# Expert routing and the last sums of a Perceiver block on one core: filler products between the counts, ranks in PSUM, earlier last adds and writes

## The chip, the cores and the metric

The kernel runs on one core of a Trainium2 chip. The metric is the device time of one execution in microseconds, the median of several runs. The profile is one execution of its own, recorded by the hardware profiler; its times are given from the start of the span.

## The reference

The reference takes two latents of 256 rows and 256 channels each (512 tokens in all) and two contexts of 4096 rows of 128 channels, in float32. Six layers follow each other, each with a residual: cross attention, a state-space layer, a spectral layer, a second cross attention, a sparse self attention, and a mixture of experts. The change lies in the last of them:

```python
x = x + _L1_ffn_ref(_layernorm(x, axis=-1), L1_ffn_W1, L1_ffn_W2, L1_ffn_Wr)

E, DFF, TOPK = (8, 1024, 2)
logits = jnp.einsum('btd,ed->bte', x, Wr)
probs = jax.nn.softmax(logits / TEMPERATURE, axis=-1)
topk_vals, topk_idx = jax.lax.top_k(probs, TOPK)
router_weights = topk_vals / topk_vals.sum(-1, keepdims=True)
one_hot = jax.nn.one_hot(topk_idx, E, dtype=x.dtype)
gate = jnp.einsum('btk,btke->bte', router_weights, one_hot)
h = jax.nn.silu(jnp.einsum('btd,efd->btef', x, W1))
y = jnp.einsum('btef,edf->bted', h, W2)
out = jnp.einsum('bte,bted->btd', gate, y)
```

## The kernel before

The first five layers fill the span up to about 730 us. An order written out by hand (the string `ORDER`) weaves the work of the two latents together there; while `in_order[0]` is true, calls through the wrappers `te`, `ve` and `se` (TensorE, VectorE, ScalarE) keep their program order, and the profile gives all of them the line of the wrapper, L172. The part that follows, L1313 to L1579, is mostly written with plain `nc.` calls, which a scheduler orders on each engine.

The 512 tokens lie as four tiles (`NT` = 4) of 128 rows. The router's products (`ps_r`) give eight logits for each token. The selection (L1327 to L1337) is a chain of small VectorE operations: twice the greatest logit, as a mask `sel`, and their sum `picked`, 128 x 4 x 8. For each token and expert the rank of the token among those that chose the expert is needed. TensorE multiplies `picked` by a matrix of ones (totals of a tile) and by `above`, a strict triangle (tokens ahead in the tile), both into one bank `ps_n` (L1343, L1344); VectorE adds the totals up over the tiles into `cum` (L1349) and then `pos` (L1351). `cum[:, NT, :]` is the number of tokens of each expert.

The work of the experts is cut into blocks of 128 tokens. Block k below 8 holds the first 128 tokens of expert k; further blocks hold what is over. Twelve blocks (`ALWAYS` = 12) are always worked on; three more stand under the condition at L1569, which reads `filled`, and were not needed in these runs. `direct(k)` gathers the tokens of blocks 0 to 2 by a product: a comparison of `count` with `number` makes a 0/1 matrix S of 128 x 512 (L1367), and eight products of `xn5` with it give the block, turned (`ps_xs`, L1374). The tokens of all blocks are also scattered to `x_slots` in DRAM by eight indirect DMAs on GpSimd's queue (L1406), at places computed by VectorE (`slot`, `two`, `both`, `at`). From block 3 on, ScalarE's queue fetches a block from there (L1454) and TensorE turns it (L1459).

Each block goes through `hidden` (`ps_h`, L1466, with Silu on ScalarE at L1473) and `output` (`ps_y`, L1482). The results of blocks 0 to 9 are stored to `y_slots` (L1491); those of blocks 10 and 11 stay on the core and are spread over the tokens by products with `SHARES` (`combine`, L1515, added to x by VectorE at L1520). After block 9, `collect` reads each token's two results back with eight indirect DMAs on GpSimd's queue (L1527), and VectorE adds each row to x with its weight (L1531). The weights of the experts come on SyncE's queue (L1262, L1263). The last four DMAs write x out, two on SyncE's queue and two on ScalarE's (L1579); they stand behind the condition.

## Time and profile before

| what | value |
|---|---|
| time, median of 3 runs (lowest to highest) | 852.71 us (852.42 to 853.16) |
| the profiled execution: its own time, its span | 855.07 us, 853.3 us |
| granted TensorE clock, mean of the span | 0.979 |
| busy: PE, PEld, DVE, ACT, POOL | 801.2, 572.7, 581.5, 451.8, 46.3 us |
| share of the chain that ended last: PE, DVE, ACT | 82%, 10%, 4% |
| router's last product ends; selection's last mask starts | 738.57 us; 741.28 us |
| direct products, 48 instructions | 744.71 to 752.73 us |
| first of eight gathers starts; last one starts | 834.62 us; 843.48 us |
| writes of x issued from | 848.98 us |

PE is TensorE's products, PEld its loads of weights, DVE is VectorE, ACT ScalarE, POOL GpSimd, SP SyncE; a "q" behind a name is the engine's queue, which also issues DMAs. One product of 128 x 128 weights in float32 shows as two instructions. Busy time tells how long an engine worked, not that it was waited for; the chain that ended last tells which work the end stood behind. "Granted clock" is the share of TensorE's full clock in a stretch.

### The profile page before, as it was taken

To read this page: it belongs to the slowest core of one execution; us is meant where nothing else is said; L and a number is where in the kernel's file an instruction comes from. 1 tells how busy PE (TensorE), PEld (TensorE's weight loads), DVE (VectorE), ACT (ScalarE), POOL (GpSimd) and SP (SyncE) were. 2 spreads that over 40 slices of the span, in tenths; PEclk is the share of its full clock that TensorE was granted. 3 is DMA by queue.
4 is the path that set the end of the run, shared out by engine and by line. 5 is a ranking of instruction groups with operands and counts; after the bars stand their busy time and mean duration, and the time that the engine had idled before them with its cause. 6 is when DMAs were issued, how large, how long until landed. Compare 5 with 4: busy or idle time off the path is not lost.

```text
span 853.3 us, 20944 instructions
## 1 busy us (share of the span) xinstructions
PE 801.2 (94%) x8596; PEld 572.7 (67%) x8596; DVE 581.5 (68%) x1072; ACT 451.8 (53%) x858; POOL 46.3 (5%) x108
## 2 busy tenths in 40 slices
PE   5998999999999999999988999989799999699996
PEld 3675666666666666666655666865668865599985
DVE  4686888887878787687798766888774587631112
ACT  6434666666666666566654787655534244311110
POOL 5004011000000000000000000000000000030003
PEclk9997999999999999999999999999999999699998
DMA  7215114001101010100000101130305502339502
GB/s 269 55 35 181 25 39 124 17 20 23 23 17 24 11 30 18 22 14 15 2 2 2 51 2 49 53 99 1 99 2 196 196 2 68 132 111 330 200 13 82
DMA packets 35313, 56.65 MB, mean 66 GB/s; under 512 B 5872, under 2 KB 22816, under 8 KB 35216
## 3 DMA queue, kind: packets, MB, share of 16 engines
q1 hardware_dynamic: 27904, 41.44, 16.0%
q0 software_dynamic: 3264, 10.05, 3.5%
q10 hardware_dynamic: 4048, 3.80, 1.6%
q8 instruction: 69, 1.13, 0.6%
q14 instruction: 28, 0.23, 0.1%
HBM read 42.16 MB, written 4.85 MB: 55 GB/s over the span
## 4 chain that ended last, share of the span: by engine, by line
PE 82%; DVE 10%; ACT 4%; issue 2%; DMA 1%; POOL 1%; POOLq 0%; ACTq 0%; DVEq 0%
PE ps L172 29%; PE av L172 17%; PE ps_h L1466 5%; PE ps_y L1482 4%; PE ps_k L172 4%; PE ps_v L172 3%; PE ps_s L172 3%; DVE mp L172 3%; DVE states L172 2%; PE ps_aqk L172 2%; PE ps_in L172 2%; PE ps_pt L172 1%; PE ps_f L172 1%; PE ps_ht L172 1%; PE asc L172 1%
## 5 line engine op out<-in xcount | busy, mean ns | idle before, releaser
L172 DVE TENSOR_REDUCE mp<-ps 128x2 f32<-128x1024 f32 (+1 forms) x273 | 303.1, 1153 | 96.7 <-PE ps L172 96.6
L172 ACT ACTIVATE exps<-ps 128x512 f32<-128x512 f32 x512 | 266.6, 602 | 131.0 <-PE ps L172 130.7
L172 PE MATMUL ps<-qk,KB 32*128 32x256 f32 x2048 | 260.7, 397 | 3.4 <-ACT exps L172 1.7
L172 PE MATMUL ps<-KB,qk 32*128 32x256 f32 x2048 | 251.4, 395 | 4.5 <-DVE mp L172 4.5
L172 PEld LDWEIGHTS ps<-KB,qk 32*128 32x128 f32 x2048 | 172.9, 186 | 60.2 <-issue 34.0
L172 PEld LDWEIGHTS ps<-qk,KB 32*128 32x128 f32 x2048 | 187.8, 186 | 18.1 <-ACT exps L172 5.2
L172 PE MATMUL av<-exps,V 128*32 128x256 f32 x2048 | 136.8, 385 | 1.2 <-ACT exps L172 0.8
L172 PEld LDWEIGHTS av<-exps,V 128*32 128x32 f32 x2048 | 53.7, 109 | 63.5 <-ACT exps L172 33.2
L172 DVE TENSOR_TENSOR av<-av 128x256 f32<-128x256 f32 x120 | 49.5, 412 | 5.4 <-PE av L172 5.0
L1473 ACT ACTIVATE room<-ps_h 128x512 f32<-128x512 f32 x24 | 14.2, 597 | 72.6 <-PE ps_h L1466 51.4
L1466 PEld LDWEIGHTS ps_h<-room,w 128*128 128x128 f32 x384 | 44.5, 192 | 0.5
L1466 PE MATMUL ps_h<-room,w 128*128 128x128 f32 x384 | 44.7, 275 | 0.0
L1482 PE MATMUL ps_y<-w,room 128*128 128x256 f32 x192 | 43.3, 379 | 0.0
L172 PEld LDWEIGHTS ps_v<-l_wv,ctxT 128*128 128x128 f32 x256 | 32.6, 191 | 15.2 <-issue 6.6
L172 DVE TENSOR_TENSOR_SCAN states<-decay,ps_in 128x256 f32<-128x256 f32 x64 | 40.0, 669 | 2.5 <-PE ps_in L172 2.5
L1482 PEld LDWEIGHTS ps_y<-w,room 128*128 128x128 f32 x192 | 35.6, 190 | 4.4
L172 PE MATMUL ps_k<-ctxT,wkc 128*128 128x512 f32 x64 | 36.5, 655 | 0.0
L172 PE MATMUL av<-more,nat 128*128 128x256 f32 x128 | 33.4, 384 | 3.0 <-DVE more L172 2.8
L172 PE MATMUL ps_v<-l_wv,ctxT 128*128 128x128 f32 x256 | 35.0, 280 | 1.0 <-ACT V L172 1.0
L172 ACT COPY qk<-ps_k 128x512 f32<-128x512 f32 x32 | 18.7, 587 | 26.8 <-PE ps_k L172 25.1
L172 PE MATMUL ps_s<-ctxT,xn 128*128 128x512 f32 x64 | 29.5, 594 | 0.0
L172 ACT COPY V<-ps_v 128x512 f32<-128x512 f32 x32 | 18.8, 587 | 20.1 <-PE ps_v L172 15.1
(308 smaller groups left out, 854.6 us busy)
## 6 DMA issues: line engine op xcount, KB each, us to landing
w<-in_moe_w SPq DMA_DIRECT2D x24, 1024.0 KB, 7.6
KB<-qk SPq DMA_DIRECT2D x220, 32.0 KB, 2.0
ctxT<-in_ctxT SPq DMA_DIRECT2D x4, 512.0 KB, 7.8
ctxT<-in_ctxT POOLq DMA_DIRECT2D x4, 512.0 KB, 5.1
x_slots<-O POOLq DMA_DIRECT2D x15, 128.0 KB, 6.2
y_slots<-room ACTq DMA_DIRECT2D x10, 128.0 KB, 4.2
room<-x_slots ACTq DMA_DIRECT2D x9, 128.0 KB, 5.2
KB<-qk ACTq DMA_DIRECT2D x32, 32.0 KB, 2.2
```

Source lines behind the costliest of these rows:

```text
L172: i = getattr(self.engine, name)(*args, **kw)
L1466: nc.tensor.matmul(ps[fc // 4][:, (fc % 4) * P : (fc % 4 + 1) * P], lhsT=weights[k][0][:, c, fc * P : (fc + 1) * P], rhs=xT[k][:, c, :], s ...
L1473: nc.scalar.activation(hT[k][:, 4 * i : 4 * i + 4, :].rearrange("p f n -> p (f n)"), ps[i], AF.Silu)
L1482: nc.tensor.matmul(ps[:, :D], lhsT=hT[k][:, fc, :], rhs=weights[k][1][:, fc, :], start=(fc == 0), stop=(fc == NF - 1),)
```

## The change

Eight products of a constant row with the identity, read by nobody (`at_work(8)`), stand between the router's products and the counts, and four more (`at_work(4)`) between the counts and the direct products. The ranks are summed in PSUM: `picked` gets a fifth slice of zeros, and five products that accumulate in one bank give `pos` and the number of tokens `num` at once; `cum` and its adds are gone. S is made in four comparisons of 128 x 128 for each block in place of one of 128 x 512. These products keep their program order. At the end, `collect` issues the gathers and returns the adds; seven of the eight adds come first, then the combined results, then the eighth add, in that order on VectorE. x is written ahead of the condition, and inside it once more for the case that it is taken.

```diff
+        picked = one.tile([P, NT + 1, E], F32, tag="picked", name="picked")
+        nc.vector.memset(picked[:, NT, :], 0.0)
+        def at_work(n):
+            ps = bank("ps_work")
+            for _ in range(n):
+                te.matmul(ps[:, :D], lhsT=ident, rhs=rows[:, LN_G, :], start=True, stop=True)
...
-        nc.vector.tensor_add(picked, sel[:, 0, :, :], sel[:, 1, :, :])
-        flat = picked.rearrange("p t e -> p (t e)")
+        nc.vector.tensor_add(picked[:, :NT, :], sel[:, 0, :, :], sel[:, 1, :, :])
+        in_order[0] = True
+        at_work(8)
         ps = bank("ps_n")
-        nc.tensor.matmul(ps[:, : NT * E], lhsT=ones, rhs=flat, start=True, stop=True)
-        nc.tensor.matmul(ps[:, NT * E : 2 * NT * E], lhsT=above, rhs=flat, start=True, stop=True)
-        tot = ps[:, : NT * E].rearrange("p (t e) -> p t e", e=E)
-        cum = one.tile([P, NT + 1, E], F32, tag="cum", name="cum")
-        nc.vector.memset(cum[:, 0, :], 0.0)
+        te.matmul(
+            ps[:, : (NT + 1) * E], lhsT=above, rhs=picked.rearrange("p t e -> p (t e)"), start=True, stop=False
+        )
         for t in range(NT):
-            nc.vector.tensor_tensor(cum[:, t + 1, :], cum[:, t, :], tot[:, t, :], ALU.add)
-        pos = one.tile([P, NT, E], F32, tag="pos", name="pos")
-        nc.vector.tensor_tensor(
-            pos, cum[:, :NT, :], ps[:, NT * E : 2 * NT * E].rearrange("p (t e) -> p t e", e=E), ALU.add
-        )
+            te.matmul(
+                ps[:, (t + 1) * E : (NT + 1) * E].rearrange("p (t e) -> p t e", e=E), lhsT=ones,
+                rhs=picked[:, t : t + 1, :].to_broadcast([P, NT - t, E]), start=False, stop=(t == NT - 1),
+            )
+        at_work(4)
+        pos = ps[:, : NT * E].rearrange("p (t e) -> p t e", e=E)
+        num = ps[:, NT * E : (NT + 1) * E]
...
-            nc.vector.tensor_tensor(
-                S, count.unsqueeze(1).to_broadcast([P, NT, P]),
-                number[:, :, k : k + 1].to_broadcast([P, NT, P]), ALU.is_equal,
-            )
+            for t in range(NT):
+                nc.vector.tensor_single_scalar(S[:, t, :], count, number[:, t, k : k + 1], ALU.is_equal)
...
-                    nc.tensor.matmul(
+                    te.matmul(
                         ps[:, c * P : (c + 1) * P], lhsT=xn5[:, t, c * P : (c + 1) * P], rhs=S[:, t, :],
...
         direct(0)
-        num = cum[:, NT, :]
+        in_order[0] = False
...
-        def collect():
-            for i in range(TOP_E):
-                for t in range(NT):
+        def collect(i, t):
...
+            def added():
+                ve.scalar_tensor_tensor(x[:, t, :], row, kept[:, i, t : t + 1], x[:, t, :], ALU.mult, ALU.add)
+            return added
...
-                collect()
+                rows_of.extend(collect(i, t) for i in range(TOP_E) for t in range(NT))
...
+        in_order[0] = True
+        for added in rows_of[:-1]:
+            added()
         combine((STORED, STORED + 1))
+        rows_of[-1]()
+        in_order[0] = False
+        write()
         with tc.If(nc.values_load(filled[0:1, :], min_val=0, max_val=E - 1) > ALWAYS - E):
...
             blocks(ALWAYS, NB, add_up)
-        for t in range(NT):
-            (nc.scalar if t % 2 else nc.sync).dma_start(out=out[t * P : (t + 1) * P, :], in_=x[:, t, :])
+            write()
```

## The prediction

> **What bounds the kernel now.** I read the page first. In it the chain that ended last is PE for 82% of the span, so time is won only where that chain leaves PE at full speed, or at its ends. The change touches two places: the routing (about 738 to 753 us) and the last ten microseconds. The next view is the chain of waits in order of time for 736 to 775 us (start, length, what):

> ```profile
> 741.61 0.61 PE ps_n L1343 x2
> 742.22 0.44 PE ps_n L1344 x2
> ...
> 743.96 0.60 DVE gathered L1367
> ...
> 744.71 8.01 PE ps_xs L1374 x48
> 752.73 7.15 PE ps_h L1466 x64
> 759.87 3.46 PE ps_y L1482 x16
> ```

> DVE picks the experts until 741.5 us, PE counts for 1.05 us, DVE ranks and compares for 2.0 us, and from 744.71 us PE is the chain. Its first 48 instructions (the direct products, 128 columns) take 8.01 us, or 167 ns each; the 64 behind them, of the same shape, take 112 ns. The view by windows says why (columns: stretch, length, busy time of PE, PEld, DVE, ACT, POOL, then the granted clock, DMA share, GB/s):

> ```profile
> 732.00:734.00 2.00, 1.17 (x6) 1.12 (x7) 1.61 (x6) 0.20 (x1) 0.00 (x0) 0.68 0.41 131
> ...
> 748.00:749.00 1.00, 1.00 (x7) 1.00 (x6) 0.43 (x2) 0.00 (x0) 0.00 (x0) 0.50 0.00 0
> 749.00:750.00 1.00, 1.00 (x8) 1.00 (x8) 0.90 (x7) 0.00 (x0) 0.00 (x0) 0.61 0.00 0
> 750.00:751.00 1.00, 1.00 (x12) 1.00 (x10) 0.14 (x3) 0.00 (x0) 0.67 (x1) 1.00 0.00 0
> ```

> What follows the routing, from the timeline (start, length, engine, line, operation):

> ```profile
> 749.87 0.17 DVE L1402 CAST at<-both 128x8 int32<-128x8 f32 x1
> ...
> 750.33 1.05 POOL L1406 DMA_INDIRECT x_slots<-xn,at  x1 [83.52 <-DVE known L1448]
> ...
> 762.20 1.32 ACTq L1454 DMA_DIRECT2D room<-x_slots  x3
> ...
> 766.74 0.38 PE L1459 MATMUL ps_xs<-ident,room 128*128 128x128 f32 x2
> ```

> The scatters start when the slots are known, the fetches on ACT's queue wait for all eight, and PE needs the first fetched block at 766.74 us. And the end:

> ```profile
> 845.13 0.48 DVE L1531 SCALAR_TENSOR_TENSOR x<-gathered,kept,x 128x256 f32<-128x256 f32 x1 [0.82 <-DMA gathered<-y_slots,known]
> 847.09 0.48 DVE L1531 SCALAR_TENSOR_TENSOR x<-gathered,kept,x 128x256 f32<-128x256 f32 x1 [1.48 <-DMA gathered<-y_slots,known]
> 847.49 1.41 DVE L1520 TENSOR_TENSOR x<-x,ps_c 128x256 f32<-128x256 f32 x4
> 848.98 0.85 SPq L1579 DMA_DIRECT2D out_x<-x  x2
> 848.99 0.88 ACTq L1579 DMA_DIRECT2D out_x<-x  x2
> ```

> The eighth gathered row sets the end; the four combined adds wait behind it although their products were done at 845.45 us; then four writes, two on each queue.

> **Routing, step by step.** (1) The eight products stand on PE directly behind the router's, which end at 738.57 us. Each is two instructions of 256 columns: 16. At full clock ps_y shows 3.46/16 = 0.216 us for one, at half clock 0.43 (the 256-wide scores between 73.6 and 76.3 us, at clock 0.50, stand 0.43 apart). On this run's grid the next full step is 739.54 to 742.96 us, so 4.4/0.43 = 10.2 instructions are slow and 5.8 x 0.216 = 1.25 us fast: PE is free at 744.2 us. The selection that this work lies beside ends at 741.5 us, so 2.7 us stick out on the path.

> (2) The ranks: five products, ten instructions of at most 40 columns. They cost what the weight load costs, taken from warm ps_xs (its last 16 instructions, 750.98 to 752.73 us: 0.109 us each): 1.1 us, and 0.2 us until DVE sees the last: 745.5 us, against 742.66 before. Gone are the four dependent adds and the position add on DVE, 742.68 to 743.54 us.

> (3) The four products behind the ranks: 8 x 0.216 = 1.7 us, PE free at 747.0 us. Meanwhile DVE makes `number` (0.2 us) and the first four compares, now one for each tile. The nearest row is L1500, four 128x128 in 1.10 us: all four are there at 745.5 + 0.2 + 1.2 = 746.9 us, just covered; were they half as slow again, PE would wait about 0.4 us. The other eight compares alternate with eight small operations (0.26 + 0.08 us a pair), ending at 749.6 us; PE needs the third block at 747.0 + 3.5 = 750.5 us.

> (4) The direct products, all at full clock: 48 x 0.109 = 5.25 us, ending at 752.3 us against 752.73. That is -0.4 us. Where the grid falls in another execution is open: a lag of one step (3.4 us) gives -1.0, of two steps (6.8 us, all 16 slow) +0.8. With the 5.07 us that this trace shows it is -0.1. I take **-0.2**, ends -1.0 and +0.8.

> [...]

> (5) Scatters: the cast to `at` now comes behind all compares. 749.6 us + 0.9 us for slots, the xT copy, two, both and the cast gives 750.7 us against 750.04: the scatters (POOL) and the fetches (ACT's queue) go 0.6 us later, 762.8 us. Queued behind the fetches on ACT is the second block's Silu (763.57 us before); its product on PE starts at 767.1 us, so it is covered. The first fetch lands 2.0 us after issue (the shortest of nine), at 764.8 us, and PE asks for it at 766.5: covered by 1.7 us. If that cover goes, the fetch runs beside the 2 MB weight load that SP issues at 763.36 us, lands after 5.2 us (the median of the nine) at 768.0, and PE stops 1.5 us.

> From 752 to 831 us PE is without a gap but one of 1.9 us (ps_sh waiting for DVE, unchanged), so the -0.2 reaches the gathers whole; they, their queue (POOL) and their landings stay as they are.

> **The end.** Seven gathered adds, then the combined four: after the seventh (845.13 us) they start at 845.5 and end at 846.9 us, before the last row is there at 847.03. The last add runs 847.09 to 847.57 us. Writes 0 to 2 are issued at about 846.1, 846.4 and 846.7 us, behind the last gather's data; the fourth on ACT at 847.66 us with a free queue, against 849.49 for the last issue before: 1.8 us earlier. It lands 1.7 us after issue (the store of y_slots at 832.02 us, alone) to 2.3 us (the median of out_x on ACT's queue): 849.4 to 850.0 us, where SP saw the last landing at 851.90.

> Against that: SP stands in the condition's other branch behind its writes now. Before, it passed one wait for each DMA semaphore there between 793.9 and 834.0 us, covered by PE. Now the fourth write's semaphore holds these waits; about seven follow it at 0.066 us, and four more of the closing waits that were done before the landing: +0.7 us, uncovered. ACT's and DVE's reading of the flag (0.5 us each) ends before the landing. Sum: 849.5 us + 1.37 (landing to end before) + 0.7 = 851.6, against 853.27: **-1.6**, ends -1.1 (slow landing) and -2.3 (the extra waits cost nothing).

> **Sum.** -0.2 - 1.6 = -1.8 us. The profiled execution (855.07 us, span 853.3) becomes 853.3; it stands 2.36 us over the median of 852.71 us, which becomes 850.9. What a measurement here can tell from no change is 0.2%, 1.7 us, so the bound is 851.0, very near.

> **Rivals.** *The whole cold cost comes back* (0.13): the clock returns early in the eight products (-1.0) and the extra waits are cheap: -2.8 us, 849.9. For it: a full step of dense work is all the trace asks for. Against: half of the grid's positions give less.

> *One end eats the other* (0.19): a late step (+0.8), or the fetch behind the weight load (+1.5), and a landing of 2.3 us (-1.1): about -0.3, 852.4. For it: the compares are covered by 0.1 us only and the fetch by 1.7. Against: both need a row slower than the nearest one.

> *The filling products do not raise the clock* (0.08): slower. Their weights are an identity, with one product repeated; should that not count as work, 16 x 0.43 ends at 745.4 us, the ranks at 0.24 each at 747.8, four more products at 751.2, and the direct products (24 slow at 0.21, 24 fast) at 758.9 us: +6.2 - 1.6 = +4.6, 857.3. It decides from where the direct products, warm, start behind 748.7 us, as the end's 1.6 us is then spent. Against: direct products alone raised the clock in one step.

> **How the numbers follow.** The forecast has 0.60, spread over 850.0 to 851.8; about 0.42 of it lies under 851.0. With the first rival faster is 0.55; same is 0.18 + 0.19 = 0.37; slower 0.08. The range 849.7 to 852.6 leaves out the third rival and a little below.

> **What would show it.** Right: clock 1.00 before 745.4 us, 48 direct instructions in about 5.3 us from about 747, scatters near 750.9, no PE gap at the first fetched block, the last write issued alone about 0.6 us behind the last row, some 2.1 us from its landing to the end. Wrong: the clock at 0.50 in the direct products, PE waiting for compares or fetches, or the last write landing as late as before.

## The result and the profile after

The changed kernel takes 852.32 us (median of 22 runs, 849.39 to 854.87) against 852.77 us for the kernel before on the same chips (22 runs, 850.38 to 856.08). The ratio is 0.9993, with a 95% interval of 0.998 to 1.0005: no difference that this measurement can tell. The profiled execution took 854.43 us, with a span of 852.7 us.

Both kernels spread over some 5 us from run to run. In the profiles the clock falls to one half in the attention, for three steps of 3.41 us (67.12 to 77.36 us before, 67.16 to 77.40 after), and for single steps later (708.82 to 712.24 us before, 466.52 to 469.93 after). Of the 22 executions of the changed kernel the nine longest, 854.31 to 854.87 us, have a mean clock of 0.982 to 0.984, the other 13, 849.39 to 853.03 us, one of 0.985 to 0.990. The last copy of the logits, where the routing begins, lies between 733.7 and 738.7 us in the profiles. So executions are compared here by stage: the routing from the start of that copy (738.60 us before, 738.73 after), the end from the start of the eighth gather (843.48 before, 843.40 after).

The routing first: the chain of waits of the changed kernel in order of time (start, length, what).

```profile
738.69 5.75 PE ps_work L172 x16
744.44 1.01 PE ps_n L172 x10
745.45 1.83 PE ps_work L172 x8
747.28 5.36 PE ps_xs L172 x48
752.64 7.15 PE ps_h L1474 x64
```

PE never leaves the chain: 5.75 us of filler, 1.01 us of ranks, 1.83 us of filler, and then the direct products in 5.36 us where they took 8.01. The view by windows (columns as in the prediction; PEclk is the number behind the five engines) shows the clock:

```profile
742.00:743.00 1.00, 1.00 (x4) 0.73 (x4) 0.17 (x1) 0.54 (x2) 0.00 (x0) 0.50 0.06 16
743.00:744.00 1.00, 1.00 (x6) 0.90 (x5) 0.00 (x0) 0.00 (x0) 0.00 (x0) 1.00 0.00 0
...
748.00:750.00 2.00, 2.00 (x20) 2.00 (x19) 1.86 (x14) 0.00 (x0) 0.00 (x0) 1.00 0.00 0
```

Half clock until 743.0 us, full clock behind it; before, it returned at 749.78 us. The first expert product starts 13.75 us behind the logits in the trace, against 13.97 before. That is the whole of the routing: -0.2 us, and the eight gathers keep it.

The end, from the timeline (start, length, engine, line, operation):

```profile
844.99 0.48 DVE L172 SCALAR_TENSOR_TENSOR x<-gathered,kept,x 128x256 f32<-128x256 f32 x1 [0.80 <-DMA gathered<-y_slots,known]
845.39 1.41 DVE L172 TENSOR_TENSOR x<-x,ps_c 128x256 f32<-128x256 f32 x4
845.83 1.02 SPq L1577 DMA_DIRECT2D out_x<-x  x2
846.17 1.53 ACTq L1577 DMA_DIRECT2D out_x<-x  x2
846.83 0.48 DVE L172 SCALAR_TENSOR_TENSOR x<-gathered,kept,x 128x256 f32<-128x256 f32 x1
```

The combined adds now lie ahead of the last gathered add, three writes leave while it is awaited, and the fourth is issued alone, at 847.35 us in the trace. All as the change wants it. The gain is lost behind that: the waits of SP's queue (line waited at, releaser, us in total, times, longest) and the DMA view of 847 to 849.1 us, in which the fourth write is issued (queue, packets, MB, share of 16 engines; then the write with its size and the us from issue to landing):

```profile
SPq L1589 <- SPq L1589: 3.6, 2, 3.1
```
```profile
q8 instruction: 1, 0.02, 4.2%
...
out_x<-x ACTq DMA_DIRECT2D x1, 128.0 KB, 3.2
```

The write takes 3.2 us to land. Fifteen of its sixteen parts are done by 849.00 us in the trace; the sixteenth runs from 849.71 to 850.06 us. Ahead of it, one close behind the other, lie a packet of 16 KB on the queue "instruction" (from 847.62 us for 1.42 us; program code, by the queue's name and by its pace of one packet for about 256 of TensorE's instructions, below), and the last part of the third write (849.03 to 849.71 us), which is late too. The trace does not number the DMA engines; that one of the sixteen was taken by the fetch is read from this sequence. Ahead of the fetch stands TensorE's branch at the condition: it started at 843.10 us and took 3.70 us, where it took 0.375 us before; the fetch began 0.8 us behind its end. The kernel ends 9.32 us behind the eighth gather's start, against 9.79 before: -0.5 us.

### The profile page after: what moved, and what is told of

It reads as the page before. It is cut to its first block, busy times and chain, and to the rows that moved or that the text cites. A ratio compares the mean times of both kernels' runs of the same rounds, so it can differ in the third digit from the quotient of the medians.

```text
span 852.7 us, 21009 instructions
## 1 busy us (share of the span) xinstructions
PE 806.0 (95%) x8626; PEld 576.9 (68%) x8626; DVE 581.4 (68%) x1076; ACT 452.5 (53%) x858; POOL 46.3 (5%) x108
## 3 DMA queue, kind: packets, MB, share of 16 engines
HBM read 42.16 MB, written 4.85 MB: 55 GB/s over the span
## 4 chain that ended last, share of the span: by engine, by line
PE 84%; DVE 9%; ACT 4%; issue 2%; DMA 0%; ACTq 0%; DVEq 0%
PE ps L172 29%; PE av L172 17%; PE ps_h L1474 5%; PE ps_y L1490 5%; PE ps_k L172 4%; PE ps_v L172 3%; PE ps_s L172 3%; DVE mp L172 3%; DVE states L172 2%; PE ps_aqk L172 2%; PE ps_in L172 2%; PE ps_pt L172 1%; PE ps_f L172 1%; PE ps_ht L172 1%; PE ps_am L172 1%
## 5 line engine op out<-in xcount | busy, mean ns | idle before, releaser
L172 DVE TENSOR_REDUCE mp<-ps 128x2 f32<-128x1024 f32 (+1 forms) x273 | 303.2, 1154 | 97.8 <-PE ps L172 97.7
L172 ACT ACTIVATE exps<-ps 128x512 f32<-128x512 f32 x512 | 267.1, 603 | 132.3 <-PE ps L172 132.0
L172 PE MATMUL ps<-qk,KB 32*128 32x256 f32 x2048 | 261.8, 398 | 3.4 <-ACT exps L172 1.7
L172 PE MATMUL ps<-KB,qk 32*128 32x256 f32 x2048 | 252.6, 396 | 4.5 <-DVE mp L172 4.5
L172 PEld LDWEIGHTS ps<-KB,qk 32*128 32x128 f32 x2048 | 173.8, 187 | 60.7 <-issue 34.4
L172 PEld LDWEIGHTS ps<-qk,KB 32*128 32x128 f32 x2048 | 188.6, 187 | 18.4 <-ACT exps L172 5.2
L172 PE MATMUL av<-exps,V 128*32 128x256 f32 x2048 | 137.3, 386 | 1.2 <-ACT exps L172 0.8
L172 PEld LDWEIGHTS av<-exps,V 128*32 128x32 f32 x2048 | 53.8, 109 | 63.5 <-ACT exps L172 33.3
L172 DVE TENSOR_TENSOR av<-av 128x256 f32<-128x256 f32 x120 | 49.7, 414 | 5.9 <-PE av L172 5.5
L172 PEld LDWEIGHTS ps_v<-l_wv,ctxT 128*128 128x128 f32 x256 | 32.6, 191 | 15.2 <-issue 6.2
L172 DVE TENSOR_TENSOR_SCAN states<-decay,ps_in 128x256 f32<-128x256 f32 x64 | 40.0, 670 | 2.5 <-PE ps_in L172 2.5
L172 PE MATMUL ps_k<-ctxT,wkc 128*128 128x512 f32 x64 | 36.5, 655 | 0.0
L172 PE MATMUL av<-more,nat 128*128 128x256 f32 x128 | 33.4, 384 | 3.0 <-DVE more L172 2.9
L172 PE MATMUL ps_v<-l_wv,ctxT 128*128 128x128 f32 x256 | 35.0, 280 | 1.0 <-ACT V L172 1.0
L172 ACT COPY qk<-ps_k 128x512 f32<-128x512 f32 x32 | 18.7, 588 | 26.8 <-PE ps_k L172 26.5
L172 ACT COPY V<-ps_v 128x512 f32<-128x512 f32 x32 | 18.8, 587 | 20.8 <-PE ps_v L172 15.7
L172 PE MATMUL ps_s<-ctxT,xn 128*128 128x512 f32 x64 | 29.5, 594 | 0.0
```

The costliest lines, as they stand in the source:

```text
L172: i = getattr(self.engine, name)(*args, **kw)
```

## The experiments

Two theories stood at first. For the routing: the filler's own time eats what the clock gives. For the end: the order is right, and something about the new program makes the last write land late. The rivals were that the filler is worth the 2.6 us that the slow direct products cost before, and that a write behind the gathers takes 3 us in any case. One execution each, except where an interval is given.

**The filler taken out.**

```diff
-        at_work(8)
...
-        at_work(4)
```

> The changed kernel without its twelve filler products (nothing of the result is left out). Read from the copy of the last logits to the first ps_h, 14.1 us before and 13.9 us after. Theory (the filler gives back what it wins): the ranks start at once behind the selection, at half clock: 10 instructions x 0.22 + 0.2 = 2.4 us, the direct products start some 6.0 us behind the logits and run slow for about 5 us: 14.0 us in all, within 0.9 us (where the clock's grid falls), and the clock is 0.50 when they start. Rival (the filler is worth the 2.6 us that the slow direct products cost before): 1.5 us or more longer than after. The end of the kernel is as after.

Time 853.40 us. The first expert product starts 13.90 us behind the logits (with filler 13.75): by this pair the filler is worth 0.15 us. That is no more than executions differ by: the kernel with 12 products at the start (below) has this routing without filler too and shows 13.64 us. The direct products took 7.91 us, at half clock until 749.71. And the end, expected to stay as it was, came at 8.31 us behind the eighth gather, a full microsecond earlier than with filler, with the same instructions there. TensorE's branch took 0.375 us, no 16 KB fetch ran behind the last add, and SP's wait was short:

```profile
SPq L1587 <- SPq L1587: 2.6, 2, 2.2
```

So the filler in the routing costs the end 1 us, 100 us later.

**The second filler alone taken out.**

```diff
-        at_work(4)
```

> The changed kernel without the four filler products between the ranks and the direct products. Theory: PE waits only for number and the first compare, about 0.6 us behind the ranks in place of 1.7 us behind them: the direct products start 1.0 us sooner at full clock, and the stage is 12.9 us in place of 13.9 (plus or minus what the grid gives in the eight products, 0.9). Rival (compares or clock are the bound): with the compares the bound, the direct products stop between blocks and end where they end after, 13.9 us; with the clock the bound, it falls in the gap and they take over 6 us in place of 5.4.

Time 849.93 us. The chain of waits:

```profile
735.06 5.59 PE ps_work L172 x16
740.66 1.03 PE ps_n L172 x10
...
742.37 5.60 PE ps_xs L172 x48
747.96 7.15 PE ps_h L1473 x64
```

The first expert product starts 12.70 us behind the logits: the four products behind the ranks cost some 0.9 to 1.05 us and kept nothing up, as the clock stayed at 1.00 without them. (The ranks start 5.56 us behind the logits here and 5.71 with the change, and the eight products took 5.59 us and 5.75, so the clock may have returned a little sooner; 0.15 of the 1.05 us may be that.) So the eight products alone are worth 0.9 to 1.2 us against the two executions without filler, and the four take that back. The end stayed late (9.51 us, branch 3.96 us, landing seen 3.1 us after issue).

**The writes behind the condition again, the adds in the new order.**

```diff
         in_order[0] = False
-        write()
         with tc.If(...):
...
-            write()
+        write()
```

> The changed kernel with the writes of x behind the condition again; the order of the adds is that of the change. Read from the start of the eighth gather to the end of the span: 9.8 us before, 9.3 us after. Theory: behind the condition all four writes wait until DVE has passed it (0.7 us behind the last add's start + 0.5), go out in pairs, the last issued at 5.2 us, landing 2.4 us later, and the end 1.4 us behind that as before: 9.0 us; SP's waits of the other branch are covered again. Rival (the writes ahead of the condition are what won): 9.8 us or more.

Time 854.26 us, end 9.06 us. All four writes are issued 4.67 to 5.17 us behind the eighth gather, not when the last add is done, at 847.59 us, but when VectorE has passed the condition:

```profile
847.10 0.48 DVE L172 SCALAR_TENSOR_TENSOR x<-gathered,kept,x 128x256 f32<-128x256 f32 x1
848.09 1.25 SPq L1577 DMA_DIRECT2D out_x<-x  x2
848.09 1.26 ACTq L1577 DMA_DIRECT2D out_x<-x  x2
```

So here the reading of the flag is on the path. In the kernel before, all four writes wait behind VectorE's condition too, and the first starts at 848.98 us, though its own rows were done at 847.91. But there VectorE's branch was over at 848.49 us and the last combined add ended only at 848.90: the add was the later of the two, and the flag cost the path nothing. The end is 0.3 us earlier than with early writes: the last write lands 0.6 us later (7.67 us behind the eighth gather, not 7.10), but from there to the end it is 1.4 us in place of 2.2. The branch was slow here too (4.0 us); its fetch was over at 848.94 us, when the writes' first data went at 848.95, and the last write landed in 2.5 us.

**The condition between the combined adds and the last two gathered adds, writes behind it.**

```diff
-        for added in rows_of[:-1]:
+        for added in rows_of[:-2]:
             added()
         combine((STORED, STORED + 1))
-        rows_of[-1]()
-        in_order[0] = False
-        write()
         with tc.If(...):
...
+        for added in rows_of[-2:]:
+            added()
+        write()
```

> The changed kernel with the condition between the combined adds and the last two gathered adds, and the writes behind these. Theory (the last write of the changed kernel landed late, 3.2 us after its issue, since code fetched for the branch held one of the 16 DMA engines; and SP's waits stood behind it): the branch is over before the last write is issued, so it lands 1.7 to 2.4 us after its issue and the span ends 1.4 us behind that, in place of 2.2: 7.6 to 8.4 us from the start of the eighth gather, against 9.3. Rival (a lone last write takes 3.2 us whatever the branch does, being behind three others): 9.1 us. A second rival: DVE's reading of the flag, 0.6 to 0.8 us, pushes the last two adds so far that nothing is won: 9.0 us or more with a landing of 2 us.

A miss: 854.11 us, end 8.97 us, where 7.6 to 8.4 were expected. SP's extra waits are gone, but the last write takes 3.6 us all the same, from its issue at 847.40 us to its landing at 850.99. TensorE's branch took 3.88 us and the fetch ran still later, 5.20 to 6.15 us behind the eighth gather. The second rival falls, as the last add came only 0.1 us later (3.53 us behind the eighth gather, not 3.43). By the number alone the first rival (3 us in any case) would stand; the next runs decide.

**The change's end with the routing of before.** The new `collect`, the order of the adds and `write()`, and none of the routing:

```diff
 # the kernel before, and
+        for added in rows_of[:-1]:
+            added()
         combine((STORED, STORED + 1))
+        rows_of[-1]()
+        write()
         with tc.If(...):
```

> The kernel before with the end of the change alone (order of the adds, writes ahead of the condition); the routing is the old one, so PE's program is as long as before. Theory (code fetch: the longer PE program of the change moves the condition's target into code that is not there yet; PE's branch then takes 3.7 us in place of 0.4, and the 16 KB fetched behind it hold one DMA engine just when the last write passes): PE's branch takes 0.4 us, no 16 KB fetch starts after the last row's add, and from the start of the eighth gather to the end of the span it is 8.3 us, as without filler, against 9.8 before and 9.3 with the change. Rival (the write is late by itself; the run without filler was a lucky one): 9.3 us with a landing of 3.2 us. The stage from the logits to ps_h is 14.0 us, within 0.9, in both.

Time 851.12 us, end 8.29 us, branch 0.375 us. The DMA view of 844.8 to 846.9 us, with the last write:

```profile
q14 instruction: 2, 0.02, 3.0%
...
out_x<-x ACTq DMA_DIRECT2D x1, 128.0 KB, 2.2
```

Only two fetches of 8 KB (q14), no 16 KB on q8, and the write lands in 2.2 us. Timed in more executions:

> The same kernel as the one with the change's end alone and the routing of before, now timed. Theory (the end's order and the early writes are worth 1.5 us as long as TensorE's program is not lengthened): ratio to the kernel before 0.9975 to 0.999, the median 0.9 to 2.1 us below it, the end 8.2 to 8.4 us behind the start of the eighth gather. Rival (the 1.5 us were a matter of one execution): ratio 0.9995 to 1.0005, end 9.3 us or more.

851.41 us (12 runs) against 853.22 (17 runs): ratio 0.9972, interval 0.9958 to 0.9986. The end alone, without the routing, is a gain that can be told; by stage it is 1.5 us.

**No filler, but a program as long as with it.** Twelve products of one column at the very start, where TensorE has nothing to do (1.7 to 6.9 us):

```diff
     make_identity(nc, ident)
+    pad = bank("pad")
+    for _ in range(12):
+        nc.tensor.matmul(pad[:, :1], lhsT=ident, rhs=ident[:, :1], start=True, stop=True)
...
-        at_work(8)
...
-        at_work(4)
```

> The changed kernel without filler in the routing, but with twelve products of one column at the very start, where PE is idle: nothing runs otherwise at the end, only PE's program is as long as with the change. Theory (code fetch): PE's branch takes more than 3 us again, a 16 KB fetch starts about 4.2 us behind the eighth gather's start, and the end is 9.3 us behind it, 1.0 us more than the same kernel without these twelve (8.3). Rival (the filler itself, where it stands, made the end late, or chance): 8.3 us.

Time 851.63 us, end 9.86 us, the latest of all: 1.5 us later than the kernel that differs by these 12 products, 840 us away. The branch took 3.85 us. The DMA view with the last write, and SP's wait:

```profile
q8 instruction: 1, 0.02, 4.2%
...
out_x<-x ACTq DMA_DIRECT2D x1, 128.0 KB, 3.6
```
```profile
SPq L1590 <- SPq L1590: 4.0, 2, 3.5
```

One execution, but branch, fetch and landing all turned together: not what the filler does decides, but how many instructions TensorE has.

**Filler ahead of the router.** Five products in each of the router's two calls, six behind it, none behind the ranks:

```diff
+        early_work(5)
...
-        at_work(8)
+        at_work(6)
...
-        at_work(4)
```

> The changed kernel with ten filler products (2 x 5) ahead of the router's transposes, where PE is idle for 4.7 us, six in place of eight behind the router's products and none behind the ranks. Theory (the half clock begins in the idle time before the router, and the change fills too late): the clock stays at 1.00 from 728 us on; from the last residual sum (the idle time's start) the router's transposes and products are 1.5 us shorter, the ranks start at the end of the selection (3.0 us behind the logits in place of 5.5), and ps_h starts about 10.5 us behind the logits in place of 13.8: some 4.5 us in all, unless the fetches of block 3, now close to the weight load, stop PE by up to 2 us. Rival (small products of 8 columns and transposes do not hold the clock even so): the clock falls between 733 and 740 us and ps_h starts 13 us or more behind the logits.

Time 849.23 us, end 9.47 us. Half of what was expected: the first expert product starts 12.03 us behind the logits, not 10.5. The clock was up until 740.83 us and fell for one step, after one in which PE was busy for 2.35 of 3.41 us, with a gap around the ranks:

```profile
738.00:740.00 2.00, 1.25 (x10) 1.19 (x10) 0.56 (x4) 0.92 (x2) 0.00 (x0) 1.00 0.00 0
740.00:742.00 2.00, 1.91 (x12) 1.94 (x13) 1.96 (x14) 0.00 (x0) 0.00 (x0) 0.71 0.00 0
742.00:744.00 2.00, 2.00 (x11) 2.00 (x11) 0.72 (x4) 0.00 (x0) 0.00 (x0) 0.50 0.00 0
```

With the early condition as well:

```diff
         early_work(5)
...
-        for added in rows_of[:-1]:
+        for added in rows_of[:-2]:
```

> The same filler ahead of the router, with the condition ahead of the last two gathered adds and the writes behind them. Theory: the routing as in the run with early filler; the end 7.6 to 8.4 us behind the eighth gather's start if no code is fetched there, 9.0 if it is (PE's branch over 3 us shows which): some 5 us less than the changed kernel in all. Rival: as in that run.

Time 849.01 us, end 8.97 us, branch 3.85 us and the last write again 3.6 us from issue to landing. The routing is the same (12.03 us), but the gathers start 95.71 us behind the logits instead of 94.08: the clock fell for a step at 810.57 us, about the gap before ps_sh (1.92 us long in the profiles of before and after, where it stayed at 1.00).

**Filler of 512 columns, half the instructions.**

```diff
-                te.matmul(ps[:, :D], lhsT=ident, rhs=rows[:, LN_G, :], ...)
+                te.matmul(ps, lhsT=ident, rhs=rows[:, LN_G : LN_G + 2, :]..., ...)
...
-        at_work(8)
+        at_work(4)
...
-        at_work(4)
+        at_work(2)
```

> The changed kernel with filler products of 512 columns, 4 and 2 of them, in place of 8 and 4 of 256: the same columns stream through TensorE in half the instructions, so TensorE's program grows by about 36 rows against the kernel before, not by 60. Theory (the length of TensorE's program decides whether the code behind the condition has been fetched): the routing stays as it was (first expert product 13.6 to 13.9 us behind the last copy of the logits). The end is one of two: where the branch takes 0.4 us, no 16 KB code fetch follows the last add and the kernel ends 8.2 to 8.5 us behind the start of the eighth gather; where the branch still takes 3.7 to 4.0 us, the fetch is there and the end is 9.2 to 9.5 us. 12 extra rows were short, 45 were long, so 36 may fall on either side; what would speak against the theory is a mixed result: a short branch with an end above 9.0 us, or a long one below 8.6. Rival (the filler's work itself, not its length, delays the last write): 9.2 to 9.5 us with a short branch too.

Time 853.78 us. The first expert product starts 14.02 us behind the logits, later than the 13.6 to 13.9 expected; the clock returned 4.85 us behind the logits here, 4.27 with the change. The end is the mixed result that the text calls evidence against the theory: a branch of 0.37 us, and an end at 9.60 us. But the place of the loss is another one. From the last add's start to the end it is 4.74 us, as in the two kernels without filler (4.9 us), where the change has 5.9. What is late is the last add itself, at 4.86 instead of 3.43 us: the seventh gather landed 1.4 us late. The DMA view of 841 to 845.2 us has the cause:

```profile
q0 software_dynamic: 144, 0.39, 32.8%
q8 instruction: 1, 0.02, 2.0%
```

The fetch that follows the branch now ran from 0.36 us behind the eighth gather's start for 1.33 us, across the gathers (q0); fifteen of the seventh gather's sixteen parts had landed by 1.45 us, the sixteenth at 2.92, and the seventh add started at 3.01 us where it starts at 1.57 with the end alone.

**The same with the first filler only.**

```diff
-        at_work(2)
```

> The changed kernel with its first filler as 4 products of 512 columns and without the second filler: TensorE's program is about 28 rows longer than before. Theory: the routing behaves as with the first filler alone (first expert product 12.5 to 13.0 us behind the last copy of the logits; before 13.97, with both fillers 13.75). The branch takes 0.4 us. The code fetch that follows it then falls in the time of the last gathers: where it shares no DMA engine's turn with the seventh or eighth gather, the last add starts 3.4 to 3.6 us behind the eighth gather's start and the end is 8.2 to 8.4 us behind it; where it does, as it seems to have done with 36 rows more, the last add comes 1.0 to 1.6 us later and the end is at 9.2 to 9.8 us. From the last add's start to the end it is 4.7 to 4.9 us either way (5.9 us in the changed kernel). Ratio to the kernel before 0.9955 to 0.9985. Rival (the end's 8.3 us are to be had only without filler): from the last add to the end 5.6 to 6.0 us, ratio 0.998 to 0.9995.

851.62 us (10 runs) against 852.77 (13 runs): ratio 0.9981, interval 0.9969 to 0.9993. The first expert product starts 12.90 us behind the logits, the branch took 0.375 us, and it is 4.70 us from the last add to the end. The end is at 8.61 us, between the two forecasts: the last add started at 3.91 us, as the seventh gather landed 0.5 us late beside a fetch. Of the routing's 1.1 us nothing reaches the gathers, though: they start 96.25 us behind the logits, against 96.02 before. The DMA view of 828.4 to 831.4 us:

```profile
q8 instruction: 1, 0.02, 1.9%
issues: line engine op xcount, KB each, median us to landing
y_slots<-room ACTq DMA_DIRECT2D x1, 128.0 KB, 3.0
```

A code fetch again, at a third place: beside the last store to y_slots, for which the gathers wait. It landed in 3.0 us instead of the 1.7 that the prediction read off the kernel before; the gathers began 1.3 us later than they could.

The traces tie these fetches to TensorE's place in its program. "Rows" counts TensorE's instructions in the trace beyond those of the kernel before; the fetch near the last store is given from that store's issue:

| rows more | kernel | fetch near the last store | branch | last write: issue to SP's seeing it land |
|---|---|---|---|---|
| 0 | the end alone (two executions) | +2.17, +2.17 us | 0.375 us | 2.19, 2.13 us |
| 12 | no filler | +1.95 | 0.375 | 2.20 |
| 29 | 512 columns, first filler | +0.88 | 0.375 | 1.99 |
| 37 | 512 columns, both | +0.05 | 0.369 | 2.02 |
| 45 | first filler | -1.20 | 3.955 | 3.13 |
| 59 | no filler, same length | -2.34 | 3.852 | 3.59 |
| 61 | the change | -2.35 | 3.695 | 3.17 |
| 76 | filler ahead of the router | -3.10 | 3.955 | 3.14 |

More rows move the fetch near the store earlier, by 0.07 us for each on the average of all 76, though unevenly from one kernel to the next. Between 37 and 45 rows the branch turns slow, and one more fetch, 0.8 to 1.0 us behind its end, falls beside the last write. Below that this fetch is absent; the two that remain run about the store and about the last gathers. The three kernels with the condition or the writes moved (61, 61 and 76 rows) have slow branches too, 3.85 to 4.01 us.

The runs show fetches of 16 KB, one for about 256 rows (below), and a branch that takes ten times as long in some kernels (3.70 to 4.01 us against 0.37); that the branch waits for a fetch is the author's reading, and no trace shows it directly. Transfers beside a fetch took up to 1.5 us longer: the last part of the seventh gather came 1.47 us behind the other fifteen with 37 rows more, and the last store to y_slots took 3.0 us in place of 1.7 with 29.

**A version of all this.** Filler of 128 columns ahead of the router (8 in each call), 13 behind it, 5 behind the ranks, 9 in the gap before ps_sh; the early condition; and one-column products, 11 at the start and 8 ahead of the condition, that only make the program 257 rows longer than before. The kernel before has 17434 such rows in its trace and 69 fetches on q8. From the first fetch (23.5 us) to the 68th (834.2 us) there are 17138 rows, or 255.8 for each of the 67 steps: some 256 rows more should bring the fetches back to where they were.

```diff
     make_identity(nc, ident)
+    for _ in range(11):
+        nc.tensor.matmul(pad[:, :1], lhsT=ident, rhs=ident[:, :1], start=True, stop=True)
...
+        early_work(8)
...
-        at_work(8)
+        at_work(13)
...
-        at_work(4)
+        at_work(5)
...
+            if k == STORED + 1:
+                for _ in range(9):
+                    nc.tensor.matmul(ps[:, :P], lhsT=ident, rhs=m[1][:, 0, :], start=True, stop=True)
```

> A version made of what the experiments point to: filler of 128 columns ahead of the router (8 products in each of its calls), 13 behind the router, 5 behind the ranks, 9 while TensorE waits for the shared expert's products; the condition ahead of the last two gathered adds and the writes behind it; and 11 one-column products at the start and 8 ahead of the condition, which only bring TensorE's program to a length of about 260 rows more than before, one code block of 256 rows and 4. Theory: the clock stays at 1.00 through the routing and the first expert product starts 10.0 to 11.0 us behind the last copy of the logits (before 13.97); the branch takes 0.4 us again, no 16 KB fetch runs beside the last writes and the kernel ends 7.4 to 8.1 us behind the eighth gather's start (before 9.79); in all 5 to 8 us less than before, ratio 0.990 to 0.994. Rival 1 (the branch is slow for any longer program): end 8.9 to 9.1 us, ratio 0.992 to 0.996. Rival 2 (the clock falls for a step in the routing whatever is done there): first expert product at 12.0 us or later, ratio 0.993 to 0.997.

845.71 us (6 runs, 843.64 to 848.61) against 853.22: ratio 0.991, interval 0.9882 to 0.9937. The windows:

```profile
734.00:736.00 2.00, 2.00 (x19) 2.00 (x19) 0.87 (x6) 0.00 (x1) 0.00 (x0) 1.00 0.00 0
...
738.00:740.00 2.00, 1.94 (x17) 1.78 (x17) 0.56 (x5) 1.04 (x2) 0.00 (x0) 1.00 0.00 0
740.00:742.00 2.00, 2.00 (x20) 2.00 (x19) 2.00 (x16) 0.00 (x0) 0.00 (x0) 1.00 0.00 0
```

The clock stays at 1.00 from the router through the ranks. The first expert product starts 10.69 us behind the logits (before 13.97), the branch takes 0.375 us, and the end comes at 7.97 us (before 9.79). The 256 rows fit, and so does the fetch near the last store: 257 less the 32 rows that stand only behind it are 31 short of 256, and 31 x 0.07 us behind +2.17 is about +4.3, where +3.96 was seen. One expectation was missed: a 16 KB fetch did run beside the last writes, from 3.17 us for 1.25 us, and the last write landed 2.8 us after its issue. That is not one late part: all sixteen landed between 2.65 and 2.84 us, and the issues of the last two writes took 1.41 and 1.02 us where those of the change took 0.36 and 0.34. Why is not shown. Of the 3.3 us of the routing 3.1 reach the eighth gather, which with the 1.8 of the end makes 4.9 us from the logits on. From VectorE's first addition of the attention's output to x (L172, `x<-x,ps_wo`, 728.14 us before) to the end it is 118.25 us against 125.13, so 6.9 us with the router's part; the rest of the 7.5 us between the medians is within the two kernels' spread.

## Why the prediction was right or wrong

The range of 849.7 to 852.6 us holds the 852.32 measured, but near its end, and by its width: the likeliest value, 850.9, is 1.4 us too low, and what was forecast at 0.55, a gain beyond 0.2%, did not come.

*Routing, steps 1 to 4: right.* PE free at 744.2 us: the ranks began at 744.28. Ranks seen at 745.5: `number` began at 745.49. PE free at 747.0: the direct products began at 747.12. At full clock 5.25 us: 5.36. The return of the clock, at 743.00 us, fell on the step of 742.96 that was worked out. The part that was most at risk, whether products of an identity raise the clock, came out as forecast (so that rival falls). -0.2 forecast, -0.2 measured. In part that is luck, as the prediction left open where the clock's grid would fall (-1.0 to +0.8): the half clock began 5.97 us ahead of the logits with the change and 5.88 before, almost the same place. Nor is the -0.2 the filler's doing: without it the figure is -0.07 and -0.33 in two executions. With filler the direct products start 2.40 us later than in the first of these (8.39 and 5.99 us behind the logits) and take 2.55 us less (5.36 and 7.91). What step 3 did not weigh is that its four products cost more than a gap there: without them PE waited 0.7 us for the first compare, the clock stayed up, and the stage was 1.05 us shorter. The 0.43 us and 0.216 us of step 1 held as well: the filler's instructions start 0.42 to 0.43 us apart until 742.95 us, at the granted 0.50, and 0.21 to 0.22 us apart from 743.20 us on, at 1.00.

*Step 5: a small miss.* The scatters did not move by 0.6 us: 11.76 us behind the logits against 11.73. The compares and small operations alternated in 0.27 to 0.29 us a pair instead of 0.34. The cover of the first fetch was not touched, so nothing followed.

*The end: the issue right, the landing mis-sized.* The fourth write, expected at 847.66 us, went at 847.35. The extra waits of SP behind it, expected at +0.7 us, cost 0.8: from landing to end 2.2 us against 1.37. The term that failed is "1.7 us to 2.3 us" for the landing, 3.17 in fact, and with it "-1.6, ends -1.1 and -2.3", which became -0.5. With the routing that is -0.7 us by stage, and 0.45 us between the medians. Nothing in the trace of before showed a landing of 3 us there, but the prediction took the nearest stores as bounds and did not ask what else uses the DMA engines; the code fetches stand in the page's queue list and were read over. Where the fetch is absent the term is right: 2.2 us, and the end's gain is 1.5 us, with the 1.6 forecast.

*The reading of before was incomplete.* The four writes wait for the last add, as the prediction has it, but also for VectorE to pass the condition. Before, the add ended later and set the time; the run with the writes behind the condition shows the other wait, of 0.5 us behind the last add. The sum is the same, as the write's new place takes it past both.

*Rivals.* "One end eats the other" gave 852.4, and that is nearly what came, but for neither of its reasons: no late step and no fetch behind the weight load, and a landing later than its 2.3 us. So the number near it is chance. That a longer program moves code into the way was in no rival.

## What to carry to other kernels

Count the instructions that a change adds to an engine, and look at the queue list for "instruction" fetches near each transfer that the end waits for: a fetch of 16 KB beside a 128 KB store or a gather delayed its last sixteenth by about 0.5 to 1.5 us here, and a few instructions more or less moved it to another place (with 37 rows more a fetch lay beside the seventh gather, with 45 beside the last write). Filler that kept the clock up paid most where the engine would have waited anyway and was still at full clock when the path needed it (3.3 us here, with the rest of that version's routing). Put into the path while the clock was at 0.50 it paid less: eight products beside the selection brought some 1 us, and four more behind the ranks took as much away. Judge gains of a microsecond by stage, as whole executions of the changed kernel lay 5.5 us apart, the nine longest at the lowest mean clocks.

## What the runs showed that was not expected

- TensorE's branch over the condition's body took 0.37 us in kernels with 0 to 37 and with 257 rows more, and 3.7 to 4.0 us with 45 to 76. That it waits for code in the slow case is inferred from the program's length and the fetches; at which instructions the fetched pieces begin was not measured.
- A code fetch of 16 KB took 0.87 to 1.61 us (139 of them before and after), and of two transfers beside one the last of sixteen parts came late: by 1.06 us (the fourth write of the change) and 1.47 us (the seventh gather with 37 rows more). That the fetch holds one of the sixteen DMA engines is inferred from this.
- The kernel before pays for one as well: its eighth gather landed 3.52 us after its start, the other seven after 2.7 to 2.8, with a 16 KB fetch from 844.83 us for 0.96 us. In the last two kernels above the eighth gather landed after 2.71 and 2.78 us; no fetch started in its 2.7 us there.
- The clock fell after a single step of lower use, with PE still busy for 2.35 of its 3.41 us in the kernel with filler ahead of the router, and was up again a step later.
